# Keys and values between the first heads, idle products at the start, and an early output beside the last gate

## The chip, the cores and the metric

The kernel runs on one core of a Trainium2 chip. The metric is the device time of one execution in microseconds. A core has five engines with instruction queues of their own: TensorE (PE, with its weight loads PEld), VectorE (DVE), ScalarE (ACT), GpSimd (POOL) and SyncE (SP), which here issues nearly all DMAs.

## The reference

Eight sequences of 512 rows of 256 numbers go through a block of attention and a block of experts, each between two layer norms with a residual:

```python
x = x + layernorm(attn(layernorm(x), wq, bq, wkv, bkv, wo))
x = x + layernorm(ffn(layernorm(x), gate_w, w_gate, w_up, w_down, sh_gate, sh_up, sh_down))

# attn: 16 query heads of 128 in 4 groups that share keys and values
q, k = x @ wq + bq + pe, x @ wk + bk + pe
v = x @ wv + bv
out = softmax(causal(q @ k.T / sqrt(128))) @ v @ wo
# ffn: 64 experts of width 176, the 6 best of each row, at most 64 rows per expert,
#      and a shared expert of width 352 that sees every row
```

## The kernel before

All data are float32. The attention goes by heads: a loop of 128 steps k, one for each head s of each sequence b (k = 16 b + s). A step is a software pipeline over several heads, and the order of all instructions on all engines is the order in which the program writes them (a manual schedule). Each engine and SP's DMA queue go through theirs in that order.

Step k does the following, in this order:

- `scores(k, 0)` and `scores(k, 1)`: TensorE multiplies queries by keys into `psc`, VectorE masks and finds the row extremes (`e`, `least`), ScalarE takes the exponential and the row sums.
- `turned(k - 1)`: VectorE transposes the weights of the head before in 32 by 32 blocks (`eb`). SP sends them to DRAM (`ex_d`) and fetches them back as `et`, which finishes the transposition. This is called the exchange below.
- `scores(k, 2)` and `scores(k, 3)`, then `weigh(k)`: VectorE takes reciprocals, and GpSimd scales the weights.
- a place "A" for side work, `project(k - 3)` (products with `wo` into `po`), and a place "B".
- `queries(k + 1)`: TensorE computes the next head's queries into `pq`, and VectorE adds bias and positions (`qt`).
- `mix(k - 2)`: TensorE multiplies `et` by the values into `pav`, ScalarE copies (`ao`).
- for the first sequence, two steps of `zeros()` (SP fills DRAM rows with zeros), and a place "D".

`side(s, place)` runs what is put down for that place. From the second sequence on, this is the feed-forward part of the sequence before; from head 5 on the next sequence's `prepare` runs at the end of a step, a unit at a time.

`prepare(b)` yields twelve units: rows, scales and normal form of x (0 to 2), its transposition `turn` (3), `keys(g)` for four groups (4 to 7), `values(i)` for four row tiles (8 to 11). A unit of keys or values is two matrix products of 128x128 by 128x512 on TensorE and one VectorE instruction that evacuates PSUM and adds the bias. For the first sequence all twelve are run before the loop, followed by `queries(0)`:

```python
for u in prepare(0):
    u()
queries(0)
```

The loads stand at the program's head, all on SP: `x_first`, `wkv_sb`, four small ones, `wq_sb` (2 MB), `wo_sb` (2 MB) and the weights of gate and shared expert. Each DMA of SP uses one of eight completion semaphores in turn and waits for the DMA eight places ahead of it that had the same one.

The experts work in pairs during the later sequences. The outputs of the first five sequences (`EARLY`) are finished by the generator `finish_early`, in steps between heads: fetch, sum and statistics, then shift, scaling on ScalarE and the residual sum on GpSimd, then the store. `last_part(before, spare)` handles what follows the last head: the last sequence's norm, its gate (`route`: products `pg`, exponentials `sc`, the choice `chosen`, the running counts `pp`), the shared expert (`shared`), the late experts and the outputs. `spare` is what is left of `finish_early`, and `output6` is a step of the output of the sequence before the last. In the kernel before, the end of `last_part` reads:

```python
for _ in spare:
    pass
output6()
```

A loop over remaining expert pairs follows, which runs zero times on this data. It begins with all engines waiting for what is in flight.

Of the kernel before, what the change touches and what calls it, by code (L numbers as in the profile page):

```python
# [11 lines left out]
F32 = mybir.dt.float32  # L12
# [7 lines left out]
P = 128  # L20
B, T, E = 8, 512, 256
NT = B * T
NI = T // P
# [3 lines left out]
NC = E // P  # L27
G, QPG, D = 4, 4, 128
NH = G * QPG
# [6 lines left out]
NEG = -3.0e38  # L36
BIG = 3.0e38
ROW = E + NX
EARLY = 5
ET_ROWS = EARLY * T  # L40
LROW = ROW + NX

@with_exitstack
def sandwich_kernel(ctx, tc, x, wq, bq_t, wkv, bk_t, bv, wo, gate_wt, w_gate, w_up, w_down,
                    sh_gate_t, sh_up_t, sh_down_t, pe_t, out):
    nc = tc.nc
# [5 lines left out]
    ps_s = ctx.enter_context(tc.tile_pool(name="ps_s", bufs=3, space=PSUM))  # L52
# [14 lines left out]
    ident = const.tile([P, P], F32, tag="ident", name="ident")  # L67
# [54 lines left out]
    with ExitStack() as part:  # L122
# [13 lines left out]
        def load(ap, shape, name):  # L136
            t = wpool.tile(shape, F32, tag=name, name=name)
            nc.sync.dma_start(out=t, in_=ap)
            return t

        def load_x(b):
            t = p2.tile([P, NI, E], F32, tag="x", name=f"x_{b}")
            nc.sync.dma_start(out=t, in_=x[ts(b, T), :].rearrange("(i p) e -> p i e", p=P))
            return t

        x_first = load_x(0)
        wkv_sb = load(wkv.rearrange("(c p) (g k d) -> p c g k d", p=P, g=G, k=2), [P, NC, G, 2, D], "wkv_sb")
        bk_sb = load(bk_t, [D, G], "bk_sb")
        bq_sb = load(bq_t, [D, NH], "bq_sb")
        pe_sb = load(pe_t, [D, T], "pe_sb")  # L150
        bv_sb = load(bv.partition_broadcast(P), [P, G * D], "bv_sb")
        wq_sb = load(wq.rearrange("(c p) n -> p c n", p=P), [P, NC, NH * D], "wq_sb")
        wo_sb = load(wo.rearrange("(h d) e -> d h e", d=D), [D, NH, E], "wo_sb")
        gw_sb = load(gate_wt.rearrange("(c p) n -> p c n", p=P), [P, NC, NX], "gw_sb")
        sg_sb = load(sh_gate_t.rearrange("(c p) n -> p c n", p=P), [P, NC, FSH], "sg_sb")
# [56 lines left out]
        seqs = {}  # L212
# [3 lines left out]
        def prepare(b):  # L216

            s = seqs[b] = {"kt": []}

            def rows():  # L220
                s["x"] = load_x(b) if b else x_first

            def scales():
                s["scales"] = norm_scales(tiles_of(s["x"]), f"a{b}")

            def normal():
                mv, rs = s.pop("scales")
                s["xn"] = p1.tile([P, NI, E], F32, tag="xn", name=f"xn_{b}")
                for i in range(NI):
                    normalize(s["xn"][:, i, :], s["x"][:, i, :], mv, rs, i)  # L230

            def turn():
                s["xnt"] = p2.tile([P, NC, T], F32, tag="xnt", name=f"xnt_{b}")
                transpose_rows(s["xnt"], s["xn"], f"a{b}")

            def keys(g):
                pk = ps_m.tile([P, T], F32, tag="m", name=f"pk_{b}_{g}")
                for c in range(NC):
                    nc.tensor.matmul(pk, lhsT=wkv_sb[:, c, g, 0, :], rhs=s["xnt"][:, c, :],  # L239
                                     start=c == 0, stop=c == NC - 1)  # L240
                kt = p2.tile([D, T], F32, tag="kt", name=f"kt_{b}_{g}", bufs=5)
                nc.vector.scalar_tensor_tensor(kt, pk, bk_sb[:, g : g + 1], pe_sb, ALU.add, ALU.add)  # L242
                s["kt"].append(kt)

            def values(i):
                if i == 0:
                    s["v"] = p2.tile([P, NI, G * D], F32, tag="v", name=f"v_{b}")
                pv = ps_m.tile([P, G * D], F32, tag="m", name=f"pv_{b}_{i}")
                for c in range(NC):
                    nc.tensor.matmul(pv, lhsT=s["xnt"][:, c, ts(i, P)], rhs=wkv_sb[:, c, :, 1, :],  # L250
                                     start=c == 0, stop=c == NC - 1)
                nc.vector.tensor_add(s["v"][:, i, :], pv, bv_sb)  # L252

            yield rows
            yield scales
            yield normal
            yield turn
            for g in range(G):
                yield lambda g=g: keys(g)
            for i in range(NI):  # L260
                yield lambda i=i: values(i)

        def queries(k):
            b, h = divmod(k, NH)
            pq = ps_m.tile([P, T], F32, tag="m", name=f"pq_{k}")
            for c in range(NC):
                nc.tensor.matmul(pq, lhsT=wq_sb[:, c, ts(h, D)], rhs=seqs[b]["xnt"][:, c, :],  # L267
                                 start=c == 0, stop=c == NC - 1)
            qt = p2.tile([D, T], F32, tag="qt", name=f"qt_{k}")
            nc.vector.scalar_tensor_tensor(qt, pq, bq_sb[:, h : h + 1], pe_sb, ALU.add, ALU.add)  # L270
            live[k] = {"qt": qt, "e": []}
# [516 lines left out]
        def last_part(before, spare):  # L788


            b, xt, sums = B - 1, seqs[B - 1]["x"], po.pop(B - 1)
            l = {}
            shared6, output6 = before["shared"], before["output"]
            shared6()
            mv, rs = norm_scales([sums[i // 2][:, i % 2, :] for i in range(NI)], f"o{b}")
            shared6()
            shared6()
            shift = shifts(mv, rs, f"o{b}")
            two = p2.tile([P, 2, NI * E], F32, tag="v", name="o_xt2")
            o, xt2 = two[:, 0].rearrange("p (i e) -> p i e", i=NI), two[:, 1].rearrange("p (c t) -> p c t", c=NC)  # L800
            st = small.tile([P, NI, 6], F32, tag="st", name=f"st_f{b}")
            for i in range(NI):
                scale_on_act(o[:, i, :], sums[i // 2][:, i % 2, :], rs, shift, i)
                nc.vector.tensor_add(xt[:, i, :], xt[:, i, :], o[:, i, :])
                nc.vector.bn_stats(st[:, i, :], xt[:, i, :])
            mv, rs = scales_of(st, NI, f"f{b}")
            shared6()
            shared6()
            shift = shifts(mv, rs, f"f{b}")
            nc.sync.dma_start(out=rows_of(x1_d, b * T), in_=xt)  # L810
            xg = p1.tile([P, NI, ROW], F32, tag="xg", name=f"xg_{b}")
            for i in range(NI):
                if i % 2:
                    scale_on_act(xg[:, i, :E], xt[:, i, :], rs, shift, i)
                else:
                    normalize(xg[:, i, :E], xt[:, i, :], mv, rs, i)
            transpose_rows(xt2, xg, f"f{b}")
            shared6()
            r, f = route(b, xg, xt2), shared(b, xt2, l, "msmsms")
            next(r)  # L820
            shared6()
            next(r)
            next(f)
            next(r)
            next(r)
            marked = marks(table["m"], xg[:, :, E:ROW], table["places"], b, p2, "xnt")
            next(f)
            next(f)
            gather("late", [(xg, marked[0])])
            gt = turn_scores(marked[1], b, p2, "kt", 5)  # L830
            next(f)
            gate_up("late")
            next(f)
            gate_up_hidden("late")
            next(f)
            turn_hidden("late")
            next(f)
            down("late")
            py = l["py"]
            for i in range(NI):  # L840
                nc.tensor.matmul(py[i // 2][:, i % 2, :], lhsT=gt[:, ts(i, P)], rhs=pairs["late"]["dd"],
                                 start=False, stop=True, skip_group_check=True)
            shared6()
            output6()
            output6()
            mv, rs = norm_scales([py[i // 2][:, i % 2, :] for i in range(NI)], f"y{b}")
            y = p2.tile([P, NI, E], F32, tag="xnt", name=f"y_{b}")
            for n in range(2):
                nc.scalar.copy(y[:, ts(n, 2), :], py[n])
            nc.sync.dma_start(out=rows_of(ly_d, b * T - ET_ROWS), in_=y)  # L850
            shift = shifts(mv, rs, f"y{b}")
            for i in range(NI):
                scale_on_act(o[:, i, :], py[i // 2][:, i % 2, :], rs, shift, i)
                nc.vector.tensor_add(xt[:, i, :], xt[:, i, :], o[:, i, :])
                if i % 2:
                    nc.sync.dma_start(out=rows_of(out, b * T)[:, i - 1 : i + 1, :], in_=xt[:, i - 1 : i + 1, :])
            for _ in spare:
                pass
            output6()


# [8 lines left out]
                        next(rows[b])  # L870
                yield

        for u in prepare(0):
            u()
        queries(0)
        behind, ahead = {}, iter(())
        routed, zeroing = experts(), zeros()
        twice, finishing = False, False
# [1 line left out]

        def side(s, place):
            behind.pop(f"{s}{place}", lambda: None)()

        for k in range(NK):
            b, s = divmod(k, NH)
# [141 lines left out]
```

## Time and profile before

| | us |
|---|---|
| median of 3 runs | 1498.71 (1498.46 to 1499.84) |
| profiled execution, own time | 1494.35 |
| its span | 1492.6 |
| TensorE busy | 1416.8 |
| VectorE busy | 891.6 |
| ScalarE busy | 498.0 |
| GpSimd busy | 427.8 |

The profile is of one execution. Its span runs from the first to the last instruction recorded. In it, busy times of different engines overlap. The view of the whole span in 40 slices shows each engine's busy share in tenths. The timeline shows instructions in order of time, those of one kind together: start, duration, engine, line, operation, output and inputs, and in brackets the idle time ahead and what ended it. In the timeline "x4" behind a product counts matmul records: a product in float32 with 512 columns leaves two, and a unit of keys or values leaves four.

### The profile page before, as it was taken

How to read it: one execution, taken by the hardware profiler on the slowest of the kernel's cores; microseconds unless marked ns; L12 is line 12 of the kernel's file. 1: busy time of each engine (PE TensorE's matmuls, PEld its weight loads, DVE VectorE, ACT ScalarE, POOL GpSimd, SP SyncE). 2: the span in 40 equal slices, each digit the busy share in tenths (PEclk: the TensorE clock that was granted, in tenths of full speed). 3: DMA queues.
4: the chain of work that ended last, by engine and by line, in shares of the span. 5: the costliest groups of instructions: out<-in, count | busy, mean ns of one | idle time of the engine just before them, and what ended most of it. 6: DMA issues, size and time to landing. Idle time of an engine off the chain costs nothing.

```text
span 1492.6 us, 18592 instructions
## 1 busy us (share of the span) xinstructions
PE 1416.8 (95%) x5350; PEld 856.4 (57%) x5350; DVE 891.6 (60%) x3094; ACT 498.0 (33%) x1434; POOL 427.8 (29%) x682
## 2 busy tenths in 40 slices
PE   7999999999999999999999999989899999999894
PEld 3566655666656665666566656655455545565552
DVE  4565576657665676557665766666455445577442
ACT  1333343233332342233323332233323333444322
POOL 1222231124112322123112311135333354534202
PEclk9999999999999999999999999999999999999997
DMA  5764554355544464355435544459888799878611
GB/s 207 222 189 142 153 165 139 106 155 166 146 140 134 146 185 125 120 159 165 139 104 165 161 142 132 137 164 258 232 239 230 199 251 261 214 215 249 191 48 60
DMA packets 159701, 252.02 MB, mean 169 GB/s; under 512 B 16092, under 2 KB 135869, under 8 KB 159341
## 3 DMA queue, kind: packets, MB, share of 16 engines
q1 hardware_dynamic: 153453, 241.37, 54.3%
q0 software_dynamic: 6144, 9.44, 3.2%
q8 instruction: 44, 0.72, 0.2%
q14 instruction: 60, 0.49, 0.1%
HBM read 143.01 MB, written 107.74 MB: 168 GB/s over the span
## 4 chain that ended last, share of the span: by engine, by line
PE 79%; DMA 8%; DVE 7%; ACT 2%; POOL 1%; issue 1%; SPq 1%; ACTq 0%; POOLq 0%; DVEq 0%
PE pav L340 16%; PE psc L280 15%; PE pq L267 13%; PE po L352 12%; PE pk L239 4%; PE pv L250 4%; DMA ex_d<-eb 3%; PE py L684 3%; PE pgu L541 3%; PE psg L671 3%; PE psu L671 2%; DVE eb L313 2%; DMA wgu<-in_w_up 2%; PE pd L567 2%; DMA y<-y_d 1%
## 5 line engine op out<-in xcount | busy, mean ns | idle before, releaser
L297 POOL TENSOR_SCALAR e<-e,recip 128x128 f32<-128x128 f32 x508 | 266.5, 542 | 847.4 <-DVE recip L294 809.8
L287 ACT ACTIVATE e<-e,least 128x128 f32<-128x128 f32 (+3 forms) x512 | 285.9, 559 | 379.4 <-DVE least L284 372.1
L280 PE MATMUL psc<-kt,qt 128*128 128x128 f32 (+3 forms) x1024 | 309.6, 442 | 21.0 <-DVE least L284 9.9
L340 PE MATMUL pav<-et,v 128*128 128x512 f32 (+3 forms) x1024 | 296.9, 433 | 2.6 <-DMA et<-ex_d 1.8
L340 PEld LDWEIGHTS pav<-et,v 128*128 128x128 f32 x1024 | 194.4, 190 | 165.3 <-issue 122.8
L284 DVE CUSTOM_DVE_ANT_0 e<-psc,mask 128x128 f32<-128x128 f32 (+3 forms) x512 | 231.3, 479 | 52.3 <-PE psc L280 46.5
L267 PE MATMUL pq<-xnt,wq_sb 128*128 128x512 f32 x512 | 243.9, 599 | 0.0
L352 PE MATMUL po<-wo_sb,ao 128*128 128x256 f32 x1024 | 243.2, 380 | 0.7 <-ACT ao L108 0.7
L352 PEld LDWEIGHTS po<-wo_sb,ao 128*128 128x128 f32 x1024 | 192.5, 190 | 68.6 <-issue 38.2
L313 DVE STREAM_TRANSPOSE eb<-e 128x128 f32<-128x128 f32 x756 | 227.4, 364 | 0.1
L108 ACT COPY ao<-pav 128x512 f32<-128x512 f32 x128 | 75.0, 586 | 450.7 <-PE pav L340 450.7
L280 PEld LDWEIGHTS psc<-kt,qt 128*128 128x128 f32 x1024 | 164.8, 192 | 103.6 <-DVE least L284 34.0
L270 DVE SCALAR_TENSOR_TENSOR qt<-pq,bq_sb,pe_sb 128x512 f32<-128x512 f32 x128 | 95.7, 747 | 121.3 <-PE pq L267 121.2
L267 PEld LDWEIGHTS pq<-xnt,wq_sb 128*128 128x128 f32 x512 | 97.4, 193 | 70.9 <-issue 65.4
L287 ACT ACTIVATION_READ_ACCUMULATOR e<-e,least 128x1 f32 x512 | 95.8, 187 | 0.0
L294 DVE RECIPROCAL recip<-total 128x4 f32<-128x4 f32 x128 | 22.8, 178 | 119.7 <-ACT e L287 119.7
L577 POOL DMA_INDIRECT y_d<-dd,idx x32 | 51.1, 1597 | 72.8 <-ACT dd L576 48.6
L239 PE MATMUL pk<-xnt,wkv_sb 128*128 128x512 f32 x128 | 61.0, 604 | 0.0
L252 DVE TENSOR_TENSOR v<-pv,bv_sb 128x512 f32<-128x512 f32 x32 | 22.1, 692 | 64.4 <-PE pv L250 64.4
L250 PE MATMUL pv<-wkv_sb,xnt 128*128 128x512 f32 x128 | 59.7, 593 | 0.0
L541 PE MATMUL pgu<-wgu,gxt 128*64 128x352 f32 x256 | 47.6, 493 | 10.3 <-DMA wgu<-in_w_up 8.5
L242 DVE SCALAR_TENSOR_TENSOR kt<-pk,bk_sb,pe_sb 128x512 f32<-128x512 f32 x32 | 24.0, 751 | 50.2 <-PE pk L239 50.2
(191 smaller groups left out, 1090.1 us busy)
## 6 DMA issues: line engine op xcount, KB each, us to landing
ex_d<-eb SPq DMA_DIRECT2D x126, 640.0 KB
et<-ex_d SPq DMA_DIRECT2D x504, 160.0 KB
wgu<-in_w_gate SPq DMA_DIRECT2D x32, 352.0 KB
wgu<-in_w_up SPq DMA_DIRECT2D x32, 352.0 KB
wd<-in_w_down SPq DMA_DIRECT2D x32, 352.0 KB
y<-y_d SPq DMA_DIRECT2D x10, 512.0 KB
x<-in_x SPq DMA_DIRECT2D x8, 512.0 KB
x_d<-x SPq DMA_DIRECT2D x8, 512.0 KB
```

The source lines that it names most:

```text
L239: nc.tensor.matmul(pk, lhsT=wkv_sb[:, c, g, 0, :], rhs=s["xnt"][:, c, :], start=c == 0, stop=c == NC - 1)
L250: nc.tensor.matmul(pv, lhsT=s["xnt"][:, c, ts(i, P)], rhs=wkv_sb[:, c, :, 1, :], start=c == 0, stop=c == NC - 1)
L267: nc.tensor.matmul(pq, lhsT=wq_sb[:, c, ts(h, D)], rhs=seqs[b]["xnt"][:, c, :], start=c == 0, stop=c == NC - 1)
L270: nc.vector.scalar_tensor_tensor(qt, pq, bq_sb[:, h : h + 1], pe_sb, ALU.add, ALU.add)
L280: nc.tensor.matmul(psc[:, :w], lhsT=l["qt"][:, ts(i, P)], rhs=seqs[b]["kt"][h // QPG][:, :w], start=True, stop=True)
L284: nc.vector.tensor_tensor_reduce(out=e, in0=psc[:, :w], in1=mask[:, T - w :], scale=-1.0 / math.sqrt(D), scalar=BIG, op0=ALU.add, op1=ALU. ...
L287: nc.scalar.activation(e, e, AF.Exp, bias=l["least"][:, i : i + 1], scale=-1.0, accum_out=l["total"][:, i : i + 1])
L297: engine.tensor_scalar(e, e, recip[:, n : n + 1], 1.0, ALU.mult, ALU.mult)
L313: nc.vector.transpose(blocks.rearrange("p c j t -> p j c t"), l["e"][i][:, js[0] * P : (js[-1] + 1) * P].rearrange("p (j c t) -> p j c t", ...
L340: nc.tensor.matmul(pav[:, :, j:, :], lhsT=seqs[b]["v"][:, j, ts(g, D)], rhs=l["et"][:, :, AT[j] : AT[j] + NI - j, :], start=j == 0, stop=j ...
L352: nc.tensor.matmul(po[b][i // 2][:, i % 2, :], lhsT=ao[:, ts(i, P)], rhs=wo_sb[:, h, :], start=h == 0 and i % 2 == 0, stop=h == NH - 1, sk ...
L541: nc.tensor.matmul(pgu[ts(e, CAP)], lhsT=l["gxt"][:, c, ts(e, CAP)], rhs=l["wgu"][:, e, :, c, :], start=c == 0, stop=c == 1)
```

## The change

It has four parts.

1. 24 transposes of the identity are put ahead of everything else on TensorE. They need only `ident`, write a PSUM tile that nobody reads, and change no result.
2. `wq_sb` becomes four tiles of 512 KB, one for each group of heads, with a load of its own. The rows of such a load are 2 KB long, of the single load before 8 KB.
3. Before the loop only units 0 to 4 and 8 (rows, scales, normal form, turn, keys of group 0, values of tile 0) are run. The other six go to places of the first four heads: values 1 to "0B", values 2 to "0D", values 3 to "1B", keys 1 to "1D", keys 2 to "2B", keys 3 to "3B".
4. What is left of `finish_early` (shift on VectorE, four scalings on ScalarE, four sums on GpSimd, one 512 KB store on SP, all of the fifth sequence) runs ahead of the last sequence's gate, and no longer at the end.

The number of products, evacuations and bytes is otherwise the same; SP issues three loads more.

```diff
+WARM = 24
...
         x_first = load_x(0)
+
+        warm = ps_s.tile([P, T], F32, tag="s", name="warm")
+        for n in range(WARM):
+            nc.tensor.transpose(warm[:, ts(n % NI, P)], ident, ident)
...
-        wq_sb = load(wq.rearrange("(c p) n -> p c n", p=P), [P, NC, NH * D], "wq_sb")
+        wq_sb = [load(wq[:, ts(g, QPG * D)].rearrange("(c p) n -> p c n", p=P), [P, NC, QPG * D], f"wq_sb{g}")
+                 for g in range(G)]
...
-                nc.tensor.matmul(pq, lhsT=wq_sb[:, c, ts(h, D)], rhs=seqs[b]["xnt"][:, c, :],
+                nc.tensor.matmul(pq, lhsT=wq_sb[h // QPG][:, c, ts(h % QPG, D)], rhs=seqs[b]["xnt"][:, c, :],
...
             shared6()
             r, f = route(b, xg, xt2), shared(b, xt2, l, "msmsms")
+            for _ in spare:
+                pass
             next(r)
...
-            for _ in spare:
-                pass
             output6()
...
-        for u in prepare(0):
+        units = list(prepare(0))
+        rest = {"0B": units[9:10], "0D": units[10:11], "1B": units[11:12], "1D": units[5:6], "2B": units[6:7],
+                "3B": units[7:8]}
+        for u in units[:5] + units[8:9]:
             u()
         queries(0)
...
         def side(s, place):
             behind.pop(f"{s}{place}", lambda: None)()
+            if not b:
+                for u in rest.get(f"{s}{place}", ()):
+                    u()
```

More of the change, by code (lines that the diff above doesn't have):

```diff
@@ L871, in finish_early @@
                 yield
-        for u in prepare(0):
+        units = list(prepare(0))
+        rest = {"0B": units[9:10], "0D": units[10:11], "1B": units[11:12], "1D": units[5:6], "2B": units[6:7],
+                "3B": units[7:8]}
+        for u in units[:5] + units[8:9]:
             u()
         queries(0)
+        assert len(units) == 12
         behind, ahead = {}, iter(())
```

## The prediction

> **What bounds the kernel now.** The page comes first: which engine, which chain.
>
> ```profile
> PE 1416.8 (95%) x5350; PEld 856.4 (57%) x5350; DVE 891.6 (60%) x3094; ACT 498.0 (33%) x1434; POOL 427.8 (29%) x682
> ...
> PE   7999999999999999999999999989899999999894
> ...
> PE 79%; DMA 8%; DVE 7%; ACT 2%; POOL 1%; issue 1%; SPq 1%; ACTq 0%; POOLq 0%; DVEq 0%
> ```
>
> TensorE is busy 95% of the span and carries 79% of the chain. Only the first slice (7) and the last ones (8, 9, 4) have room, and the change touches just those ends. So I read the timeline there. The start:
>
> ```profile
> 8.24 2.29 PE L118 MATMUL pt_a<-ident,xn 128*128 128x128 f32 x8 [8.24 <-DVE xn L105]
> ...
> 12.23 0.33 PEld L239 LDWEIGHTS pk<-xnt,wkv_sb 128*128 128x128 f32 x1 [0.52 <-issue]
> 12.84 0.19 PEld L239 LDWEIGHTS pk<-xnt,wkv_sb 128*128 128x128 f32 x1 [0.28 <-issue]
> 13.27 0.19 PEld L239 LDWEIGHTS pk<-xnt,wkv_sb 128*128 128x128 f32 x1 [0.24 <-issue]
> ...
> 28.01 2.42 PE L280 MATMUL psc<-kt,qt 128*128 128x128 f32 x8 [0.84 <-DVE qt L270]
> ...
> 32.99 2.43 PE L280 MATMUL psc<-kt,qt 128*128 128x128 f32 x8 [0.84 <-DVE qt L270]
> ...
> 38.94 2.42 PE L280 MATMUL psc<-kt,qt 128*128 128x128 f32 x8 [1.81 <-DVE qt L270]
> ...
> 44.84 2.39 PE L340 MATMUL pav<-et,v 128*128 128x512 f32 x8 [1.76 <-DMA et<-ex_d]
> ```
>
> TensorE waits 8.24 us for the first rows. Weight loads then follow each other by 0.85 us (11.38 to 12.23), from 12.84 on by 0.43: until about 12.6 it runs at half rate. All keys and values pass before the first scores at 28.01, and the first heads then leave TensorE idle 0.84, 0.84, 1.81 and 1.76 us, since a head's VectorE-ScalarE chain is longer than its products. The end, by the timeline and by the waits of the DMA queue:
>
> ```profile
> 1475.59 1.29 SPq L856 DMA_DIRECT2D out_dram<-x  x2
> 1476.39 0.15 DVE L92 SCALAR_TENSOR_TENSOR shift_y<-mv_y,rs_y 128x4 f32<-128x4 f32 x1
> 1476.58 2.08 ACT L96 ACTIVATE y<-y,shift_y,rs_y 128x256 f32<-128x256 f32 x4 [0.57 <-DVE shift_y L92]
> 1477.26 2.77 POOL L641 TENSOR_TENSOR x<-x,y 128x256 f32<-128x256 f32 x4 [3.40 <-ACT y L96]
> 1480.05 0.92 SPq L643 DMA_DIRECT2D out_dram<-x  x2
> ```
> ```profile
> SPq L948 <- SPq L948: 3.5, 1, 3.5
> ```
>
> The last sequence's own stores are issued at 1475.59 and 1476.5. Then the early sequence's output runs alone (shift, four scalings, four sums), and two 512 KB stores follow. SP waits 3.5 us for them at the loop's entry (from 1481.5 by the trace's events, so until 1485.0); the 7.6 us left to 1492.6 are the program's close.
>
> [...] after a thin stretch the granted clock is 0.50 from 1436 to 1442.8. [...] wq's new 2 KB rows (before 8 KB) should cost nothing; x, in 1 KB rows, was landed 3.93 us after issue.
>
> **The change, part by part.**
>
> *Order at the start.* Six units (three keys, three values) leave the head of the queue. Each is four passes of 0.43 = 1.72 us: 10.3 us. Rates unchanged, query product 0 ends 10.3 us earlier, and the first scores start at 28.01 - 10.3 = 17.7. Call a head's first score S.
> - Head 0 (before 4.98 us long, 28.01 to 32.99): scores 2.26, values 1, queries, values 2 at 1.72 each = 7.42 on TensorE. VectorE has the next queries' sum ready at about S+6.7: no wait. +2.44.
> - Head 1 (before 5.95): 2.26 + 3 x 1.72 = 7.42. VectorE begins 0.34 late, behind the sum of values 2 (ready S+0.17, 0.69 long); reciprocal at S+5.4, values 3's sum, query sum ready at S+7.03: still covered. +1.47.
> - Head 2 (before 8.14): 2.26 + 1.72 + 1.72 + 2.24 = 7.94, one unit in. -0.20. The exchange must land first: eb is done at S1+3.46, the trip took 8.6 us (36.1 to 44.7), so et is there at S2+4.65; the mix asks at S2+5.70, 1.05 us later.
> - Head 3 (before 7.76, TensorE full): +1.72, no cover.
>
> Added 5.43, taken away 10.3: **-4.9 us**. Behind the six evacuations on VectorE (0.69 to 0.75 each) stand a query sum or the next mask; TensorE's unit covers them as shown. If that cover failed, each would cost up to 0.75.
>
> *wq in four loads.* SP issues three more (0.43 each), two of them behind the landings of x and wkv. Ahead of piece 0 stand 2.1 MB, with it 2.6 MB; by the DMA row of the first 80 us, 2.6 MB had moved by about 10 us. The queries now ask at about 14-15 us: 0. The whole wq would have landed near 13.6, which leaves little. SP's next duty (zeros, about 24 us) comes after its loads (last issue 18.1).
>
> *Idle products.* 24 transposes from 1.85 (ident done at 1.81). The last four of pt_a went at 0.21 us each ((10.57-9.72)/4), so they end by 7.0, before 8.24: no delay. Fully warm, the first keys' four passes (from 10.24, when ScalarE's half of xnt is there, at 0.43 each) end at 11.96, where the next unit now begins at 13.27: 1.3 saved. [...] between 7.0 and 10.2 TensorE has little, and the stretch 1432-1436, thin in the same way, did drop the clock, which could put the half rate back on the keys. Bounds: gain 1.3, loss 0.3. I take **-0.5**.
>
> *Early output beside the last gate.* Removed from the end: everything from 1476.9 to 1480.05, and one of the two last 512 KB stores. Then stores of 256, 256 and 512 KB are issued at 1475.6, 1476.5 and 1476.9. The first two were through by 1478.4; 512 KB at 335 GB/s (the rate of the last two) takes 1.6, plus 0.3-0.5 to the semaphore: SP goes on at 1480.3 instead of 1485.0: **-4.7**. At the new place the shift stands on VectorE behind hid (done 1436.9), which then idles until 1438.67. ScalarE's four scalings (2.08) fall into this gap, POOL's sums (2.77) into the 33 us ahead of its next step:
>
> ```profile
> 1439.13 0.31 ACT L380 ACTIVATE sc<-pg,most 128x64 f32<-128x64 f32 x1 [4.09 <-DVE most L376]
> ...
> 1465.47 1.01 POOL L86 TENSOR_TENSOR rs_y<-ve_y,mhalf 128x4 f32<-128x4 f32 x1 [33.40 <-DVE ve_y L84]
> ```
>
> Scalings from 1437.1 to 1439.2 may delay sc by 0.1 us; TensorE has work of its own until the pp products at 1451, chosen is ready at 1443.8: 7 us of cover, cost 0. SP's store waits for POOL until about 1440.5 with lxg_d queued behind it, which is ready only at 1442.2: 0. Without that cover it would cost up to 2.1.
>
> **Sum** against the profiled execution (span 1492.6, own time 1494.35): -4.9 - 0.5 - 4.7 = -10.1, so about 1484.2. The median shown (1498.71) is 4.4 above that execution, a difference outside both ends as far as the views show, so I carry the -10.1 over: **1488.6 us**. A measurement can tell 0.2%, 3.0 us, from nothing.
>
> **Rivals.**
> - *Idle products do nothing or hurt* [...]: -9.6 to -9.3, 1489.1 to 1489.4.
> - *The heads don't hide the units*: for the idle gaps at the first heads, against VectorE's fixed order, where a sum now stands ahead of the query sum. All 10.3 come back: 1493.5.
> - *The close doesn't move*, if GpSimd's part of it hangs on something other than the landing; SP's 3.5 us wait speaks against it: 1493.3.
> - *Slower: the exchange meets the loads.* Head 0's weights go out at about 28 us instead of 36.3. If the loads, which ended near 23, stretch through the cut of wq, every microsecond past the 1.05 of slack is TensorE's wait at the first mix. It turns the sign once the loads end later than about 39 us: 1500 and up. x's 1 KB rows speak against it.
>
> **How the numbers follow.** Forecast 0.70, idle products without use 0.12 (a number beside it), heads 0.06, close 0.05, slower 0.03, two failures together (about no change) 0.04. Faster by over 0.2%: 0.93; same 0.04; slower 0.03. Range: below 1488.6 the full warm gain (1487.8), and 2.5 us for clock dips, each 3.4 us at half rate (1.7 lost), that fall otherwise; above, it reaches to the two single failures: 1485.3 to 1493.5.
>
> **What would show it.** Right: first scores near 17 us; no idle before psc in heads 0 to 2 and none before the first pav; TensorE full to the fifth head; weight loads 0.43 apart from the first keys on (idle products); a single 512 KB store last, at 1477 less the start's shift, then a wait near 2.5 us at the loop. Wrong: a wait on wq or et among the first heads, or a query sum that TensorE waits for; a later sc that reaches pp; a close longer than 7.6 us after the last landing.

## The result and the profile after

The changed kernel takes 1493.69 us (median of 20 runs, 1485.36 to 1499.14) against 1498.8 us of the kernel before: a ratio of 0.9958, 95% interval 0.9946 to 0.9971, which is 6.3 us (4.3 to 8.1). Measured again beside another set of the kernel before it came to 0.9937 (0.9915 to 0.9959), 9.4 us. The forecast was 10.1 us faster, 1488.6 us; the first median stands 0.2 us above the upper end of its range (1493.5), while the first ratio, applied to the 1498.71 us from which the forecast started, gives 1492.4, inside it. The direction was right. The size was too large for the first measurement; the interval of the second holds it.

The page of the changed kernel, the lines that answer to those of before:

```profile
span 1492.4 us, 18642 instructions
...
PE 1422.9 (95%) x5374; PEld 861.6 (58%) x5374; DVE 891.0 (60%) x3094; ACT 498.3 (33%) x1434; POOL 427.5 (29%) x682
...
PE   8999999999999999999999999988999998898995
```

The span is the same as before (1492.6), though both ends are shorter. That is the first puzzle, and the page can't solve it. Its chain of work is of no use here either: it ends after two pieces. So I went by landmarks in the timeline. The start of the changed kernel, TensorE alone:

```profile
1.87 5.17 PE L151 MATMUL warm<-ident 128*128 128x128 f32 x24 [1.87 <-POOL ident masks.py:199]
8.22 1.73 PE L119 MATMUL pt_a<-ident,xn 128*128 128x128 f32 x8 [1.18 <-DVE xn L106]
10.19 3.62 PE L245 MATMUL pk<-xnt,wkv_sb 128*128 128x512 f32 x4 [0.24 <-ACT xnt L109]
13.64 1.88 PE L256 MATMUL pv<-wkv_sb,xnt 128*128 128x512 f32 x4
15.36 1.88 PE L273 MATMUL pq<-xnt,wq_sb 128*128 128x512 f32 x4
18.09 2.42 PE L286 MATMUL psc<-kt,qt 128*128 128x128 f32 x8 [0.85 <-DVE qt L276]
...
25.50 2.32 PE L286 MATMUL psc<-kt,qt 128*128 128x128 f32 x8
...
32.81 2.34 PE L286 MATMUL psc<-kt,qt 128*128 128x128 f32 x8
...
38.42 2.32 PE L346 MATMUL pav<-et,v 128*128 128x512 f32 x8
40.57 2.32 PE L286 MATMUL psc<-kt,qt 128*128 128x128 f32 x8
...
50.05 2.32 PE L286 MATMUL psc<-kt,qt 128*128 128x128 f32 x8
```

After the first scores at 18.09 no row has an idle time in brackets: the waits of 0.84, 1.81 and 1.76 us are gone. The heads are 7.41, 7.31, 7.76 and 9.48 us long, where the prediction had 7.42, 7.42, 7.94 and 9.48. The fifth head starts at 50.05 instead of 54.84, 4.79 us earlier.

The first keys, though, take 3.45 us (10.19 to 13.64) for their four passes, longer than before. The view of TensorE by stretches of 2 us (busy time and records, granted clock, DMA share, GB/s; the clock's record begins with its first change, at 6.7 us, and shows 1.00 ahead of it):

```profile
6.00:8.00 2.00, 1.04 (x6) 1.00 1.06 369
8.00:10.00 2.00, 1.73 (x8) 1.00 0.89 251
10.00:12.00 2.00, 1.81 (x2) 0.53 1.01 379
12.00:14.00 2.00, 2.00 (x4) 0.62 1.04 405
14.00:16.00 2.00, 2.00 (x6) 1.00 1.09 359
```

The idle products raised the clock at 6.7 us, and 3.41 us later, at 10.1, just ahead of the first keys, it fell to half until 13.5. Before the change the same four passes took 2.91 us (10.36 to 13.27), since there the clock rose at 12.6.

The end of the changed kernel, timeline and waits of the DMA queue:

```profile
1440.78 2.08 ACT L97 ACTIVATE y<-y,shift_y,rs_y 128x256 f32<-128x256 f32 x4 [2.37 <-DVE shift_y L93]
1441.51 2.77 POOL L647 TENSOR_TENSOR x<-x,y 128x256 f32<-128x256 f32 x4 [6.22 <-issue]
...
1443.16 0.31 ACT L386 ACTIVATE sc<-pg,most 128x64 f32<-128x64 f32 x1 [0.31 <-DVE most L382]
...
1479.78 1.29 SPq L864 DMA_DIRECT2D out_dram<-x  x2
1481.49 0.37 SPq L649 DMA_DIRECT2D out_dram<-x  x1
```
```profile
SPq L962 <- SPq L962: 2.9, 2, 1.8
```

The moved scalings end 0.31 us before sc, which waits for VectorE's `most` as it did before: the new place costs nothing. From the last sequence's first own store to the moment when GpSimd enters its closing drain, by the trace's events, it takes 6.07 us (1479.78 to 1485.85), before 10.42 (1475.59 to 1486.01).

### The profile page after: what moved, and what is told of

Read it like the earlier page. It is cut to its first block, busy times and chain, and to the rows that moved or that the text cites. A ratio compares the mean times of both kernels' runs of the same rounds, so it can differ in the third digit from the quotient of the medians.

```text
span 1492.4 us, 18642 instructions
## 1 busy us (share of the span) xinstructions
PE 1422.9 (95%) x5374; PEld 861.6 (58%) x5374; DVE 891.0 (60%) x3094; ACT 498.3 (33%) x1434; POOL 427.5 (29%) x682
```

## The experiments

Theory: the parts add up, -4.8 us at the start and -4.1 at the end; the idle products are worth nothing because the clock falls again. The rivals are named in the expectations. Measured, all of them together (us; "stage" is from the scores of the 97th head to those of the last, "gate" from the first weight load or product of pg to the last pp product, "close" from the first own store to GpSimd's closing drain; ratio to the kernel before, with its interval):

| kernel | ratio | first scores | fifth head | stage | gate | close |
|---|---|---|---|---|---|---|
| before | | 28.01 | 54.84 | 431.1 | 16.27 | 10.42 |
| changed | 0.9958 (0.9946-0.9971) | 18.09 | 50.05 | 439.6 | 17.10 | 6.07 |
| units_only | 0.9968 (0.9950-0.9985) | 18.60 | 50.56 | 436.9 | 16.28 | 9.65 |
| output_only | 0.9966 (0.9950-0.9981) | 27.95 | 54.81 | 438.2 | 17.16 | 6.31 |
| units_and_output | 0.9944 (0.9917-0.9970) | 18.27 | 50.23 | 435.1 | 17.33 | 6.06 |
| idle_only | 1.0019 (0.9999-1.0038) | 28.14 | 54.78 | 434.9 | 16.28 | 10.46 |
| changed_again | 0.9937 (0.9915-0.9959) | 18.07 | 50.04 | 434.4 | 12.95 | 6.06 |
| no_idle_again | 0.9942 (0.9913-0.9972) | 17.92 | 49.88 | 433.9 | 16.28 | 6.07 |
| idle36 | 0.9942 (0.9919-0.9964) | 16.38 | 48.34 | 441.8 | 16.27 | 6.06 |
| gate_fill | 0.9899 (0.9872-0.9926) | 17.80 | 49.76 | 432.7 | 12.95 | 6.04 |
| all_fill | 0.9925 (0.9904-0.9946) | 16.57 | 48.53 | 438.8 | 12.95 | 6.07 |
| whole_wq | (1499.14 us, one time) | 18.23 | 50.19 | 441.9 | 17.09 | 6.31 |

**units_only**: the spread of units with the four loads of wq, the rest as before.

```diff
-        warm = ps_s.tile([P, T], F32, tag="s", name="warm")
-        for n in range(WARM):
-            nc.tensor.transpose(warm[:, ts(n % NI, P)], ident, ident)
...
-            for _ in spare:
-                pass
             next(r)
...
+            for _ in spare:
+                pass
             output6()
```

> The kernel before with only the spread of the six units and the four loads of wq; no idle products, the output at the old place. The traces of before and after have the first scores 9.9 us earlier and the fifth head 4.8 us earlier. Theory 1, the parts add: the fifth head comes 4.8 us earlier (4.3 to 5.5), the 97th head (k = 96) as much, and the time falls by about 5 us. Rival 2, the transfer-bound stage of the experts gives the lead back: the 97th head is 5 us earlier, the time falls by under 2 us. Rival 3, the early output gains nothing in most executions: the time falls by 5 us here, and by under 1.5 us with the output alone.

The fifth head comes 4.28 us earlier, the 97th 4.22, and the time falls by 0.32%, 4.8 us (2.2 to 7.5). The lead is smaller than in the changed kernel's trace because the clock rose at 14.3 us in this execution and at 12.6 in that of before; 1.7 us more at half rate cost 0.8 us. Theory 1 holds, at the lower edge of its 4.3 to 5.5 us. The lead at the 97th head is what both theories expect; against rival 2, which expects under 2 us, speaks the time alone, with 2.2 us as its lower end. That a smaller part of the lead is lost in the experts' stage is not excluded: the stage took 437.2 us on average in the nine traces with the spread and 434.8 in the three without, and single traces scatter by more than this difference.

**output_only**: the kernel before with `spare` run ahead of the gate's first step and not at the end.

> The kernel before with only the early output moved beside the last gate. From the last sequence's first own store to the landing of the last store the traces show 9.45 us before and 5.4 us after. Theory 1: this stretch is 5.4 us here too, and the time falls by 4 us. Rival 2 (the experts' stage gives leads back) expects the same 4 us, since nothing follows that could take it. Rival 3 (the early output gains nothing in most executions): under 1.5 us.

The close takes 6.31 us, and the time falls by 0.34%, 5.1 us (2.8 to 7.5). This excludes rival 3. The gate's stretch is 0.9 us longer than before, and in the changed kernel too; that looked like a price of the new place; what is found under gate_fill below speaks against it.

**units_and_output**: the changed kernel without the three lines of `warm`; **no_idle_again** is the same once more, **changed_again** the changed kernel beside it.

> The changed kernel without its idle products. Theory 1: the sum, about 9 us faster than before; the fifth head 4.8 us earlier, as with the idle products, within 0.5 us, because the clock that they raised at 6.7 us fell again at 10.1 us. Rival 2: 4 to 5 us. If the idle products themselves cost time (through the clock), this kernel is faster than the changed kernel by 1 us or more; if they are worth what was forecast, it is 0.5 us slower.

> The changed kernel once more, beside the next one. So far: changed 0.9958 [0.9946, 0.9971] of before, without idle products 0.9944 [0.9917, 0.9970], idle products alone 1.0019 [0.9999, 1.0038]. If the idle products are neutral, both come out alike, at about 0.9943 (spread of units and output at the start and the end, -4.4 and -4.2 us by the traces). If they cost time that the start does not show, this one is 2 us or more behind the next.

> The changed kernel without its idle products, once more. Neutral: 0.9943, within 1 us of the changed kernel. Costly: 2 us or more ahead of it. Stretch from the last sequence's first own store to GpSimd's closing drain 6.1 us, as in the three kernels with the early output, against 9.7 to 10.5 us in the three without.

The two ends add: 0.9944 and 0.9942, some 8.5 us. By the first ratios, each against its own set of the kernel before, the changed kernel (0.9958) is 2.1 us behind; measured side by side (0.9937 and 0.9942) the two are level: the idle products are neutral within what these intervals tell. In the trace the first scores stand at 18.09 and 18.07 us with them, at 18.60, 18.27, 17.92 and 17.80 (units_only, these two, gate_fill) without: 0.1 us earlier with them on average.

**idle_only**: the kernel before with the 24 idle products.

> The kernel before with only the 24 idle products. In the changed kernel's trace the clock rose at about 6.7 us, after a stretch of idle products alone, and fell at 10.1 us, so that the first keys ran at half rate. [...] Theory 1: the first scores between 26.7 and 28.5 us (before 28.01), time within 1 us of before. [...] If they warm the clock for good: first scores at 26.7 us, 1.3 us faster.

```profile
6.00:8.00 2.00, 0.75 (x6) 1.00 0.97 309
8.00:10.00 2.00, 1.69 (x7) 0.88 0.91 300
10.00:12.00 2.00, 2.00 (x5) 0.50 0.96 406
```

In this view of TensorE by stretches (columns as above) the clock falls again at about 9.8 us; the trace's record has the rise at 6.1, the fall at 9.5 and the next rise at 12.9. First scores at 28.14 us, against 28.01: no gain. The time, +2.8 us (-0.1 to +5.7), can't be told from none. In this execution the clock also stood at half rate for 10 us from 869.7 on, just after TensorE had waited 2.27 us between two scores; at the 89th head this execution was 6.5 us behind that of before. In the trace of before the same wait was 1.04 us, and the clock did not fall.

**idle36**: `WARM = 36` in the changed kernel.

> The changed kernel with 36 instead of 24 idle products. [...] 24 products end at 7 us [...] (the rate fell again at 10.1 us and at 9.5 us); 36 reach to about 8 us[...]. Expected: the rise between 5.3 and 8.7 us, no fall after it, first keys at 0.43 us a pass, first scores between 16.3 and 17.5 us (18.1 in the changed kernel, 18.3 without idle products), the fifth head about 1.2 us earlier than in the changed kernel. Rival, transposes raise the clock but cannot hold it: a fall 3.4 us after the rise here too, first scores at 18 us.

```profile
1.87 6.89 PE L151 MATMUL warm<-ident 128*128 128x128 f32 x36 [1.87 <-POOL ident masks.py:199]
8.60 1.28 PE L119 MATMUL pt_a<-ident,xn 128*128 128x128 f32 x8
10.12 1.99 PE L245 MATMUL pk<-xnt,wkv_sb 128*128 128x512 f32 x4 [0.24 <-ACT xnt L109]
11.94 1.88 PE L256 MATMUL pv<-wkv_sb,xnt 128*128 128x512 f32 x4
13.66 1.88 PE L273 MATMUL pq<-xnt,wq_sb 128*128 128x512 f32 x4
16.38 2.42 PE L286 MATMUL psc<-kt,qt 128*128 128x128 f32 x8 [0.84 <-DVE qt L276]
```

TensorE's timeline shows the full effect: four passes of keys in 1.82 us, first scores 1.7 us earlier than with 24, the fifth head at 48.34. The clock rose at 7.5 us and held, though idle products and transposes were all that TensorE had until 10.1. The clearest case is all_fill, also with 36: its clock rose at 6.3 us, and the 3.41 us behind the rise end at 9.73, before the first keys at 10.31. Here are that stretch and the one behind it, and for comparison the 3.41 us between rise and fall in the changed kernel:

```profile
6.32:9.73 3.41, 3.24 (x24) 1.00 0.98 293
9.73:13.15 3.42, 3.18 (x11) 1.00 1.03 384
```
```profile
6.69:10.10 3.41, 2.08 (x11) 1.00 0.98 299
```

The first stretch of all_fill holds transposes alone, and the clock stayed at 1.00 behind it: in this trace transposes raised the clock and held it. With 24 TensorE was busy for 2.08 us of the stretch and not 3.24, and the clock fell to half at its end. The time of idle36 (0.9942, beside 0.9937 for the changed kernel) does not show the 1.7 us, which is less than its interval can tell. Its profiled execution was the slowest of eight (1498.51 us): a fall of the clock at 864 us had cost 4 us of its lead by the 89th head, and its stage of the experts took 441.8 us.

**gate_fill**: units_and_output with idle products into a PSUM tile of their own beside the last gate.

```diff
-            transpose_rows(xt2, xg, f"f{b}")
+            idle = ps_m.tile([P, T], F32, tag="m", name="idle")
+            def fill(n):
+                for j in range(n):
+                    nc.tensor.transpose(idle[:, ts(j % NI, P)], ident, ident)
+            fill(12)
+            for c in range(NC):
+                pt = ps_s.tile([P, T], F32, tag="s", name=f"pt_f{b}_{c}")
+                for i in range(NI):
+                    if c == 0:
+                        fill((0, 4, 0, 3)[i])
+                    nc.tensor.transpose(pt[:, ts(i, P)], xg[:, i, ts(c, P)], ident)
+                (on_act, on_dve)[c](xt2[:, c, :], pt)
+            fill(4)
```

> The changed kernel without idle products at the start, but with 23 of them in the thin stretch beside the last gate: 12 ahead of the transposes of the normal form, 4 and 3 between them, 4 ahead of the gate's products. In all six traces the clock is at half rate there for two or three windows (6.8 or 10.2 us), and from the gate's first product to the last pp product it takes 16.3 or 17.2 us. [...] no fall there, and that stretch takes about 13 us, the whole kernel 3 to 4 us faster than without the filling. Rival, the fall comes from something else than the thin stretch: the half rate stays, and the filling costs up to 1 us.

TensorE by stretches in the changed kernel, where the gate's products begin at 1438.45:

```profile
1434.00:1436.00 2.00, 0.50 (x2) 1.00 0.75 262
1436.00:1438.00 2.00, 1.51 (x7) 0.72 0.00 0
1438.00:1440.00 2.00, 1.73 (x8) 0.50 0.00 0
1440.00:1442.00 2.00, 2.00 (x11) 0.50 0.01 4
1442.00:1444.00 2.00, 2.00 (x8) 0.50 0.00 0
1444.00:1446.00 2.00, 2.00 (x7) 0.50 0.37 131
1446.00:1448.00 2.00, 2.00 (x8) 0.72 0.78 278
```

and in gate_fill, where they begin at 1431.80:

```profile
1428.00:1430.00 2.00, 1.78 (x17) 1.00 0.56 194
1430.00:1432.00 2.00, 1.99 (x18) 1.00 0.00 0
1432.00:1434.00 2.00, 1.89 (x17) 1.00 0.01 4
1434.00:1436.00 2.00, 2.00 (x11) 1.00 0.00 0
```

With the gap filled there is no fall, in this trace and in that of all_fill, and the gate takes 12.95 us in both. In ten traces without the filling it took 16.27 to 16.28 five times (half rate for 6.8 us), 17.09 to 17.33 four times (10.2 us) and 12.95 once (changed_again, no fall). In the four traces with 10.2 us the fall came 0.8 to 1.3 us after the first transpose there, in the five with 6.8 us it came 3.1 to 3.6 us after it: the later fall went with the shorter half rate. In the changed kernel it fell at 1436.9, while the moved scalings begin at 1440.8, so they didn't cause it. All four long falls are in kernels with the moved output, but two such kernels (no_idle_again and idle36) have the short fall and the same 16.27 to 16.28 us as the three without it, so the moved work adds nothing by itself; whether it makes the long fall likelier, seven traces against three do not show. The time: 0.9899, 15 us faster than before and 6.4 us by the ratios ahead of no_idle_again; 3.4 us are the mean price of the fall in those ten traces, the rest lies within the intervals.

**all_fill**: both fillings, 36 idle products at the start and 23 beside the gate.

> The changed kernel with 36 idle products at the start and the 23 beside the last gate: the sum of the two. First scores at about 16.4 us, fifth head at about 48.3 us, no half rate beside the gate (first gate product to last pp product 13 us). Against before: -6.3 at the start, -4.2 at the close, -3 to -4 at the gate: about 14 us, ratio 0.990 to 0.991. If the filling beside the gate gains only in executions [...], 0.992.

The landmarks do as expected (16.57, 48.53, 12.95), the ratio 0.9925 is above the 0.990 to 0.991 expected, whose upper end lies inside its interval. It stands nearest to the 0.992 of the rival, that the filling gains only in some executions (the changed kernel's two traces have half rate there for 10.2 us and for none); the times do not decide between the two. The intervals of gate_fill and all_fill overlap; both medians are ahead of the changed kernel in its first measurement, and whether the 1.5 us at the start add to the other filling is not resolved by the times.

**whole_wq**: idle36 with wq in one load and one tile.

> The changed kernel with 36 idle products and wq in one load of 2 MB as before. First queries are asked at 13.7 us with the idle products holding the clock. The prediction put the landing of the whole wq near 13.6 us and that of its first quarter near 10. If so, TensorE waits here for up to 1 us or not at all: first scores between 16.4 and 17.4 us. If the split is worth nothing: 16.4.

```profile
12.03 1.88 PE L255 MATMUL pv<-wkv_sb,xnt 128*128 128x512 f32 x4
15.40 1.99 PE L272 MATMUL pq<-xnt,wq_sb 128*128 128x512 f32 x4 [1.49 <-DMA wq_sb<-in_wq]
18.23 2.43 PE L285 MATMUL psc<-kt,qt 128*128 128x128 f32 x8 [0.84 <-DVE qt L275]
```

TensorE's timeline has the first queries waiting 1.49 us for wq, which was there at about 15.4, not 13.6. First scores at 18.23, where idle36 had 16.38. In the changed kernel the queries start at 15.36, so by this landing the split is worth next to nothing there (an estimate; a run of the changed kernel with wq whole was not made). Its gain was seen with the clock held, in idle36: 1.85 us at the first scores.

## Why the prediction was right or wrong

**The spread of the units: right.** -4.9 us forecast, -4.3 to -5.1 in the four kernels with the spread and without idle products at the start (mean -4.7). The working by heads held to 0.2 us each, with VectorE's evacuations covered and et on time. That the sum came out so close is in part luck, since two misses work against each other. The four heads grew by 5.1 us together, not 5.4. The first scores came 9.4, 9.7, 10.1 and 10.2 us earlier (units_only, units_and_output, no_idle_again, gate_fill), not 10.3: the clock rose 1.7, 1.0, 0.5 and 0.2 us later than in the trace of before, and half of that is what is missing each time. The prediction's "rates unchanged" did not hold in these executions; at equal rates its 10.3 us comes out.

**wq in four loads: cost 0, as said; the landing was wrong.** Bytes moved by 13.6 us are not yet a landed load. By the semaphore events of the traces the whole wq landed at 14.7 us before the change and at 15.4 in whole_wq, 1.1 and 1.8 us later than read from the bytes; the first quarter landed at 11.0 in the changed kernel, where "about 10" was read, and the last at 15.2, between those two, so no cost of the shorter rows, estimated at 0 in the prediction, shows.

**Idle products: mis-sized.** -0.5 forecast, -0.1 found. The step that failed was to take a value near the middle of the bounds, although the case of the lower one (idle products end by 7.0, next to nothing until 10.2, the clock falls) was worked out beside it, with its example in the trace of before: TensorE busy for 2.33 of the 4 us from 1432, half rate from 1435.9. It is what both traces with 24 in the changed kernel and idle_only show, falls at 10.1, 10.1 and 9.5. So its signs failed too: first scores at 18.1, not near 17, and weight loads of the first keys 0.85 us apart, not 0.43. The rival "do nothing or hurt" was the true case: transposes alone did raise the clock, at 6.7 us, but it fell again at 10.1.

**Early output: right, 0.6 too large.** -4.7 forecast. The close is 6.04 to 6.31 us with it, 10.42, 9.65 and 10.46 without: -4.1 on average. Two terms of the sum were small: the last store went out 1.71 us after the first own one (1.3 forecast), and landed 3.7 us after its issue (3.4). No cost at the new place: right.

**The sum, and the time.** -4.7, -0.1 and -4.1 make -8.9. The first measurement, 6.3 us (4.3 to 8.1), misses it by less than 1 us at its near end; the second, 9.4 (6.2 to 12.7), has it inside, and so do both of the changed kernel without idle products. What the first one lacks, 2.6 us at its middle, stays open; the scatter of the experts' stage, told next, is large enough for it.

**The equal spans.** Not foreseen: I took the profiled execution's distance to the median (4.4 us) for something outside both ends, and that it was. The stage of the experts took 431.1 us in that execution and 432.7 to 441.9 in the eleven others, with the same instructions in the same order; that of the changed kernel drew 439.6. Its 8.5 us, with 0.8 us more at the gate, ate both gains in the comparison of spans. TensorE's busy time in this stage (columns as above) and the largest of its waits there (total, times, longest), each first before and then after, show where the time lay:

```profile
969.98:1401.09 431.11, 407.32 (x1765) 0.98 0.82 229
964.70:1404.31 439.61, 408.07 (x1765) 0.97 0.81 224
```
```profile
PE pgu L541 <- DMA wgu<-in_w_up: 8.5, 5, 2.5
PE pgu L547 <- DMA wgu<-in_w_up: 14.8, 7, 3.9
```

TensorE was idle for 23.8 us of the stage before and for 31.5 after, and most of the difference is waiting for `wgu`, the experts' weights. Without the idle time, and without half of the time at half rate (20.5 us of it before, in six falls of 3.41 us; 23.9 after, in three of 3.41 and two of 6.83), the stage is 395.6 to 397.6 us long in all twelve traces. So what differs from execution to execution is how long TensorE waits, above all for these loads (8.5 to 19.7 us, least in the trace of before), and how often the clock falls. Why the loads come later in one execution than in another stays open; the kernels without the spread have 8.5, 14.7 and 19.5 us of this wait, so the change is not needed for it.

**Rivals.** Heads that don't hide, a close that doesn't move, an exchange that meets the loads: none came (no TensorE wait among the first heads after the first scores, close 4 us shorter, no wait of pav for et).

## What to carry to other kernels

Moving ready work out of the way of a first result, into gaps whose length is read off the timeline, gives a gain that can be counted head by head; do it by landmarks, since an unrelated stage can swing by twice the gain between two executions. How far idle products for the clock reach decided their use here: 24 that ended at 7.0 us, 1.2 us ahead of the first transposes of x, gained nothing, 36 gained 1.7 us at the first scores. Look for thin stretches elsewhere too, since a further 3.4 us (on average by the traces) lay beside the last gate, where the change did not look.

## What the runs showed of the hardware

- Transposes alone raised TensorE's clock and held it: in the changed kernel it rose at 6.7 us, when TensorE had run nothing but transposes since 1.87, and in all_fill it stayed at 1.00 behind a stretch of transposes alone (6.32 to 9.73 us, busy for 3.24). All 154 times between two changes of the clock in the twelve traces are whole multiples of 3.413 us (in that of before from 3.413 to 989.865).
- The clock fell although TensorE was not idle: at the start it fell behind stretches of 3.41 us in which TensorE was busy for 1.85, 2.08 and 2.11 us by its records (idle_only, changed, changed_again), and held behind stretches with 2.69, 3.17 and 3.24 us (whole_wq, idle36, all_fill). Busy time by the records does not settle it, though: later in the kernel the clock also stayed up behind 3.41 us with as little as 1.51 us busy (units_and_output, up to 1348.2 us), and beside the last gate it stayed at 0.50 while TensorE's records are busy all the time (1440 to 1446 us in the changed kernel, above). What decides it was not shown.
- GpSimd's closing drain took 5.30 us in all twelve traces, with the early output at its old place and at the new one: the earlier last store did not shorten it.
